# A field-pair product kernel: w loaded in 16 KB rows and turned on TensorE, columns split over both array halves, first three tiles interleaved, five stores a tile

One core of one Trainium2 chip. The metric is the device time of one execution in microseconds (us), the median of several; lower is better.

## The reference

```python
# inputs: (4096, 32, 64) float32, W: (496, 64, 64) float32
idx_i, idx_j = np.triu_indices(32, k=1)          # 496 pairs i < j
vi = inputs[:, idx_i, :]
vj = inputs[:, idx_j, :]
vidots = jnp.einsum('bpd,pde->bpe', vi, W)
return vidots * vj                               # (4096, 496, 64) float32
```

The output is 520 MB; the inputs x and w are 33.6 MB and 8.1 MB. The kernel is above all a stream of stores.

## The kernel before

The batch lies on the partitions, 128 samples a tile, 32 tiles. A field i has 31 - i pairs, so one i is a [64] x [64, (31 - i) * 64] product and a multiply with a contiguous slice of x. Fields 2k and 2k + 1 lie in the two halves of the contraction rows. w is loaded with d on the partitions, so that its contiguous pieces are rows of 64 floats (256 B).

```python
opool = ctx.enter_context(tc.tile_pool(name="opool", bufs=4))
psum = ctx.enter_context(tc.tile_pool(name="psum", bufs=4, space=bass.MemoryType.PSUM))
# ... w of field 2k in partitions 0-63 and of field 2k + 1 in 64-127
eng.dma_start(
    out=wt[s * D : (s + 1) * D, :n, :],
    in_=w[p0[i] : p0[i] + n].rearrange("p d e -> d p e"),
)
# ... for each tile t, group g of field couples, couple k
nc.tensor.matmul(
    ps[:, a : a + m, :],
    xT[t][s * D : (s + 1) * D, k, :],
    wts[k][s * D : (s + 1) * D, c0 + a : c0 + a + m, :],
    start=True, stop=True,
)
# ...
nc.vector.tensor_mul(
    ot[:, o : o + n, :], ps[:, :n, :], xs[t][:, j : j + n, :]
)
# ... once a group
nc.sync.dma_start(
    out=out[t * P : (t + 1) * P, base : base + total, :],
    in_=ot[:, :total, :],
)
```

Of the kernel before, what the change touches and what calls it, by code (L numbers as in the profile page):

```python
# [1 line left out]

# [5 lines left out]

F32 = mybir.dt.float32


@with_exitstack
def kernel(
    ctx: ExitStack,
    tc: tile.TileContext,
    x: bass.AP,
    w: bass.AP,
    out: bass.AP,
):
    """out[b, p, :] = (x[b, i, :] @ w[p]) * x[b, j, :], p running over the pairs i < j.  # L20

    The batch lies on the partitions. The pairs of one i are contiguous in w and
    out, and their j are contiguous in x, so one i is one [64] x [64, (31 - i) * 64]
    product and one elementwise multiply. Fields 2k and 2k + 1 sit in the lower and
    upper half of the contraction rows, whose matmuls run side by side.
    """
    nc = tc.nc

    B, F, D = x.shape
    P = 128  # L30
    assert 2 * D == P and F % 2 == 0 and B % P == 0
    NT = B // P
    NK = F // 2
    BANK = 512 // D  # pairs in one PSUM bank
    CH = 2 * BANK  # pairs in one PSUM tile
    p0 = [i * (F - 1) - i * (i - 1) // 2 for i in range(F)]  # first pair of field i

    # Runs of field couples that share a store.
    groups, run = [], []
    for k in range(NK):  # L40
        n = p0[2 * k + 1] - p0[2 * k] + (F - 2 - 2 * k)
        if run and sum(m for _, m in run) + n > 2 * F + 2:
            groups.append(run)
            run = []
        run.append((k, n))
    groups.append(run)
    cap = max(sum(m for _, m in g) for g in groups)

    const = ctx.enter_context(tc.tile_pool(name="const", bufs=1))
    xpool = ctx.enter_context(tc.tile_pool(name="xpool", bufs=3))  # L50
    xtpool = ctx.enter_context(tc.tile_pool(name="xtpool", bufs=2))
    opool = ctx.enter_context(tc.tile_pool(name="opool", bufs=4))
    psum = ctx.enter_context(tc.tile_pool(name="psum", bufs=4, space=bass.MemoryType.PSUM))

    ident = const.tile([P, P], F32, tag="ident", name="ident")
    make_identity(nc, ident)

    def load_x(t: int):
        xs = xpool.tile([P, F, D], F32, tag="xs", name=f"xs_{t}")
        nc.scalar.dma_start(out=xs, in_=x[t * P : (t + 1) * P])  # L60
        return xs

    def transpose_x(t: int, xs):
        xT = xtpool.tile([P, NK, P], F32, tag="xT", name=f"xT_{t}")
        for h in range(NK // 8):
            pt = psum.tile([P, 8, P], F32, tag="ps", name=f"pt_{t}_{h}")
            for c in range(8):
                k = 8 * h + c
                nc.tensor.transpose(pt[:, c, :], xs[:, 2 * k : 2 * k + 2, :], ident)  # L69
            nc.scalar.copy(xT[:, 8 * h : 8 * h + 8, :], pt)  # L70
        return xT

    xs = {0: load_x(0)}

    # w of field 2k in partitions 0-63 and of field 2k + 1 in 64-127.
    wts = []
    for k in range(NK):
        wt = const.tile([P, F - 1 - 2 * k, D], F32, tag=f"w{k}", name=f"w_{k}")
        for s in range(2):
            i = 2 * k + s  # L80
            n = F - 1 - i
            if n:
                eng = nc.sync if s == 0 else nc.scalar
                eng.dma_start(  # L84
                    out=wt[s * D : (s + 1) * D, :n, :],
                    in_=w[p0[i] : p0[i] + n].rearrange("p d e -> d p e"),
                )
        wts.append(wt)

    xs[1] = load_x(1)  # L90
    xT = {0: transpose_x(0, xs[0])}

    for t in range(NT):
        if t + 2 < NT:
            xs[t + 2] = load_x(t + 2)
        for g, grp in enumerate(groups):
            if g == len(groups) // 2 and t + 1 < NT:
                xT[t + 1] = transpose_x(t + 1, xs[t + 1])
            base = p0[2 * grp[0][0]]
            total = sum(m for _, m in grp)  # L100
            ot = opool.tile([P, cap, D], F32, tag="ot", name=f"ot_{t}_{g}")
            for k, _ in grp:
                for c0 in range(0, F - 1 - 2 * k, CH):
                    live = []
                    for s in range(2):
                        n = min(CH, F - 1 - 2 * k - s - c0)
                        if n > 0:
                            ps = psum.tile([P, CH, D], F32, tag="ps", name=f"ps_{t}_{k}_{c0}_{s}")
                            live.append((s, n, ps))
                    for a in range(0, CH, BANK):  # L110
                        for s, n, ps in live:
                            m = min(BANK, n - a)
                            if m > 0:
                                nc.tensor.matmul(  # L114
                                    ps[:, a : a + m, :],
                                    xT[t][s * D : (s + 1) * D, k, :],
                                    wts[k][s * D : (s + 1) * D, c0 + a : c0 + a + m, :],
                                    start=True,
                                    stop=True,
                                )  # L120
                    for s, n, ps in live:
                        i = 2 * k + s
                        o = p0[i] + c0 - base
                        j = i + 1 + c0
                        nc.vector.tensor_mul(  # L125
                            ot[:, o : o + n, :], ps[:, :n, :], xs[t][:, j : j + n, :]
                        )
            nc.sync.dma_start(
                out=out[t * P : (t + 1) * P, base : base + total, :],
                in_=ot[:, :total, :],  # L130
            )
        del xs[t], xT[t]


# [1 line left out]
_INS = ["r_inputs", "L0_rec_W"]  # L136
_OUTS = [((4096, 496, 64), "float32")]


# [20 lines left out]
```

## Time and profile before

The time before was 1375.78 us, median of three (1375.63 to 1375.88). Its profile:

| | before |
|---|---|
| span of the profiled run | 1374.4 us |
| TensorE busy | 1282.8 us (93%) |
| VectorE busy | 1170.1 us (85%) |
| ScalarE busy | 64.9 us |
| instructions; TensorE matmul records | 13,479; 5,376 |
| first store issued | 53.5 us |
| store, issue to landing (median, 300 to 1250 us) | 11.2 us |
| VectorE's last multiply ends | 1365.6 us |

TensorE has the highest share, and that misleads: a busy share is an average, and an engine that is always handed work in time can look busy without setting the end. The pair to read is the rate of the DMA engines over time and the tile time. A *tile time* in this text is the distance between the same instruction in two successive tiles; averages over tiles 8 to 28 are taken from VectorE's first multiplies. It was 41.28 us. The DMA share adds up the times of all packets, so it can be over 1: it was 1.35 between 10 and 40 us in this kernel, which means that packets of one engine overlap in time.

### The profile page before, as it was taken

Reading aid. Unit: us, or ns where it says so; the run is one execution under the profiler, and the core shown is the slowest. Engines: PE = TensorE matmul, PEld = TensorE weight load, DVE = VectorE, ACT = ScalarE, POOL = GpSimd, SP = SyncE. Lnnn points to the kernel's source line nnn. Section 1 sums busy time; section 2 is a strip of 40 time slices with the busy share of each in tenths; the row PEclk is TensorE's granted clock in tenths of the full one; section 3 lists DMA queues with packets and bytes.
Section 4 is the critical chain, followed back from the end, with each engine's and each line's share of the span. In section 5 each row is a group of like instructions: output and inputs, shape, how many; then the busy total and the mean of one; then the engine's idle time right before and its main releaser. Section 6 shows DMA issues by size and latency. Waiting matters only on the chain.

```text
span 1374.4 us, 13479 instructions
## 1 busy us (share of the span) xinstructions
PE 1282.8 (93%) x5376; PEld 646.9 (47%) x5376; DVE 1170.1 (85%) x1472; ACT 64.9 (5%) x65; POOL 0.7 (0%) x6
## 2 busy tenths in 40 slices
PE   1699999999999999999999999999999999999997
PEld 0344444544444545444545444544444544444543
DVE  0588888998898898898888888988888988888987
ACT  0100000000000000000000000000000000000000
POOL 0000000000000000000000000000000000000000
PEclk6799999999999999999999999999999999999999
DMA  9999999999999999999999999999999999999999
GB/s 213 295 392 419 432 419 420 421 419 418 429 421 420 420 421 416 431 416 418 420 417 398 431 419 420 422 420 418 430 416 420 419 418 418 430 415 420 404 393 386
DMA packets 82990, 562.65 MB, mean 409 GB/s; under 512 B 37872, under 2 KB 37872, under 8 KB 41968
## 3 DMA queue, kind: packets, MB, share of 16 engines
q1 hardware_dynamic: 62720, 524.31, 92.5%
q10 hardware_dynamic: 20208, 37.49, 7.7%
q8 instruction: 42, 0.69, 0.2%
q14 instruction: 20, 0.16, 0.0%
HBM read 41.68 MB, written 520.09 MB: 409 GB/s over the span
## 4 chain that ended last, share of the span: by engine, by line
PE 78%; DVE 12%; DMA 5%; ACTq 2%; issue 2%; ACT 0%; DVEq 0%
PE ps L114 74%; DVE ot L125 12%; PE pt L69 4%; DMA out_dram<-ot 4%; ACTq L84 2%; DMA w<-in_L_rec_W_dram 1%; ACT xT L70 0%; ACTq L60 0%; ACT L70 0%; DVEq L125 0%; DVEq L156 0%
## 5 line engine op out<-in xcount | busy, mean ns | idle before, releaser
L125 DVE TENSOR_TENSOR ot<-ps,xs 128x1024 f32<-128x1024 f32 (+15 forms) x1472 | 1170.1, 866 | 195.5 <-PE ps L114 192.4
L114 PE MATMUL ps<-w,xT 64*128 64x512 f32 (+6 forms) x4864 | 1217.4, 540 | 75.9 <-DVE ot L125 40.1
L114 PEld LDWEIGHTS ps<-w,xT 64*128 64x128 f32 x4864 | 590.5, 186 | 689.3 <-DVE ot L125 426.9
L70 ACT COPY xT<-pt 128x1024 f32<-128x1024 f32 x64 | 63.6, 1013 | 1199.8 <-PE pt L69 1160.2
L69 PE MATMUL pt<-ident,xs 128*128 128x128 f32 x512 | 69.6, 284 | 6.4 <-DMA xs<-in_r_inputs_dram 6.3
L69 PEld LDWEIGHTS pt<-ident,xs 128*128 128x128 f32 x512 | 56.4, 143 | 28.9 <-DVE ot L125 22.6
L70 ACT ACT_TABLE_LOAD x1 | 1.3, 1283 | 42.4 <-DMA w<-in_L_rec_W_dram 42.4
masks.py:199 POOL TENSOR_SCALAR_AFFINE_SELECT ident<-ident 128x128 f32<-128x128 f32 x1 | 0.3, 292 | 0.1
masks.py:197 POOL MEMSET ident<- 128x128 f32 x1 | 0.2, 204 | 0.3 <-POOLq L147 0.3
L147 POOL MEMSET const-bfloat16-1.0<- 128x1 bf16 x1 | 0.1, 101 | 0.0
L147 POOL MEMSET const-uint8-127<- 128x1 uint8 x1 | 0.1, 101 | 0.0
L147 POOL MEMSET const-float32-0.0<- 128x1 f32 x1 | 0.1, 98 | 0.2 <-issue 0.2
L147 POOL MEMSET const-float32-1.0<- 128x1 f32 x1 | 0.1, 98 | 0.0
## 6 DMA issues: line engine op xcount, KB each, us to landing
out_dram<-ot SPq DMA_DIRECT2D x32, 2016.0 KB, 10.8
out_dram<-ot SPq DMA_DIRECT2D x32, 1984.0 KB, 9.2
out_dram<-ot SPq DMA_DIRECT2D x32, 1952.0 KB, 10.5
out_dram<-ot SPq DMA_DIRECT2D x32, 1824.0 KB, 11.0
out_dram<-ot SPq DMA_DIRECT2D x32, 1696.0 KB, 11.4
out_dram<-ot SPq DMA_DIRECT2D x32, 1568.0 KB, 11.6
out_dram<-ot SPq DMA_DIRECT2D x32, 1440.0 KB, 11.8
out_dram<-ot SPq DMA_DIRECT2D x32, 1312.0 KB, 9.8
```

The lines of the kernel that those rows point to most:

```text
L69: nc.tensor.transpose(pt[:, c, :], xs[:, 2 * k : 2 * k + 2, :], ident)
L70: nc.scalar.copy(xT[:, 8 * h : 8 * h + 8, :], pt)
L84: eng.dma_start(out=wt[s * D : (s + 1) * D, :n, :], in_=w[p0[i] : p0[i] + n].rearrange("p d e -> d p e"),)
L114: nc.tensor.matmul(ps[:, a : a + m, :], xT[t][s * D : (s + 1) * D, k, :], wts[k][s * D : (s + 1) * D, c0 + a : c0 + a + m, :], start=True, ...
L125: nc.vector.tensor_mul(ot[:, o : o + n, :], ps[:, :n, :], xs[t][:, j : j + n, :])
L147: nc = _bacc.Bacc("TRN2", target_bir_lowering=False, num_devices=1)
```

## The change

The change has these parts:

- w comes with pairs on the partitions (16 KB rows, four chunks of up to 128 pairs) and TensorE turns it. VectorE, GpSimd and ScalarE first copy the columns apart with a stride (for the later chunks GpSimd alone).
- The even and odd halves of the array no longer hold two fields, but the two halves of the columns e of one field; so one multiply serves a whole field, and any run of fields can share a store.
- Five stores a tile, of 90 to 106 pairs each, replace the smaller groups; three output buffers instead of four, three PSUM buffers instead of four.
- The first three tiles are taken block by block in turn, so that w is needed more slowly while it arrives.
- x of tiles 1 and 2 is loaded on SyncE's queue, behind the first chunk of w; x of later tiles on ScalarE's, asked for at the end of the tile whose buffer it takes.

```diff
+    def load_w(c: int):
+        raw[c] = rpool.tile([P, D * D], F32, tag="raw", name=f"raw_{c}")   # one buffer
+        nc.sync.dma_start(out=raw[c][: b - a, :], in_=wflat[a:b])
+    def turn_w(c: int, k: int, copy):
+        src = raw[c][:r, :].rearrange("p (d h e) -> p e h d", h=2, d=D)
+        copy(rp[:r], src[:, k * EP : (k + 1) * EP])
+        if k == E2 // EP - 1 and c + 1 < len(wrows):
+            load_w(c + 1)
+        # ... 8 transposes by nc.tensor.transpose, 2 evictions by nc.scalar.copy
...
-    opool = ctx.enter_context(tc.tile_pool(name="opool", bufs=4))
+    opool = ctx.enter_context(tc.tile_pool(name="opool", bufs=3))
...
+    groups = [[(0, 3)], [(3, 5), (5, 7)], [(7, 9), (9, 11)], [(11, 14), (14, 17)],
+              [(17, 20), (20, 23), (23, 26), (26, 29), (29, 31)]]
+    blocks = [(t, g) for g in range(len(groups)) for t in range(NX)]      # NX = 3
+    blocks += [(t, g) for t in range(NX, NT) for g in range(len(groups))]
...
+                for k in range(E2 // EP):      # a later chunk c of w, four parts k
+                    due.setdefault(s - 18 + 4 * k, []).append(("w", c, k))
+    engines = [nc.vector.tensor_copy, nc.gpsimd.tensor_copy, nc.scalar.copy, nc.vector.tensor_copy]
...
+                for h in range(2):
+                    rows = slice(h * D, (h + 1) * D)
+                    nc.tensor.matmul(ps[:, h, lo - pa : hi - pa, :],
+                        xT[t, r][rows, i - r[0] + 1 - h, :],
+                        wT[c][rows, lo - a : hi - a, :], start=True, stop=True)
...
+            if g == len(groups) - 1 and t + NX < NT:
+                load_x(t + NX, nc.scalar)
```

More of the change, by code (lines that the diff above doesn't have):

```diff
@@ L30 @@
     P = 128
-    assert 2 * D == P and F % 2 == 0 and B % P == 0
+    assert 2 * D == P and B % P == 0
     NT = B // P
-    NK = F // 2
-    BANK = 512 // D
-    CH = 2 * BANK
+    NP = F * (F - 1) // 2
+    E2 = D // 2
+    BANK = 512
+    CH = BANK // E2
     p0 = [i * (F - 1) - i * (i - 1) // 2 for i in range(F)]
-    groups, run = [], []
-    for k in range(NK):
-        n = p0[2 * k + 1] - p0[2 * k] + (F - 2 - 2 * k)
-        if run and sum(m for _, m in run) + n > 2 * F + 2:
-            groups.append(run)
-            run = []
-        run.append((k, n))
@@ L46 @@
-    groups.append(run)
-    cap = max(sum(m for _, m in g) for g in groups)
-    const = ctx.enter_context(tc.tile_pool(name="const", bufs=1))
-    xpool = ctx.enter_context(tc.tile_pool(name="xpool", bufs=3))
-    xtpool = ctx.enter_context(tc.tile_pool(name="xtpool", bufs=2))
-    opool = ctx.enter_context(tc.tile_pool(name="opool", bufs=4))
-    psum = ctx.enter_context(tc.tile_pool(name="psum", bufs=4, space=bass.MemoryType.PSUM))
+    groups = [
+        [(0, 3)],
+        [(3, 5), (5, 7)],
+        [(7, 9), (9, 11)],
+        [(11, 14), (14, 17)],
+        [(17, 20), (20, 23), (23, 26), (26, 29), (29, 31)],
+    ]
@@ new lines @@
+    RUN = max(b - a for g in groups for a, b in g) + 1
+    cap = max(p0[g[-1][1]] - p0[g[0][0]] for g in groups)
+    cuts = [*range(0, NP, P), NP]
+    wrows = list(zip(cuts[:-1], cuts[1:]))
+    NX = 3
+    const = ctx.enter_context(tc.tile_pool(name="const", bufs=1))
+    rpool = ctx.enter_context(tc.tile_pool(name="rpool", bufs=1))
+    ppool = ctx.enter_context(tc.tile_pool(name="ppool", bufs=2))
+    xpool = ctx.enter_context(tc.tile_pool(name="xpool", bufs=NX))
+    xtpool = ctx.enter_context(tc.tile_pool(name="xtpool", bufs=6))
@@ L55 @@
+    opool = ctx.enter_context(tc.tile_pool(name="opool", bufs=3))
+    psum = ctx.enter_context(tc.tile_pool(name="psum", bufs=3, space=bass.MemoryType.PSUM))
+    tpsum = ctx.enter_context(tc.tile_pool(name="tpsum", bufs=2, space=bass.MemoryType.PSUM))
     ident = const.tile([P, P], F32, tag="ident", name="ident")
     make_identity(nc, ident)
-    def load_x(t: int):
-        xs = xpool.tile([P, F, D], F32, tag="xs", name=f"xs_{t}")
-        nc.scalar.dma_start(out=xs, in_=x[t * P : (t + 1) * P])
-        return xs
@@ L63, in transpose_x @@
-    def transpose_x(t: int, xs):
-        xT = xtpool.tile([P, NK, P], F32, tag="xT", name=f"xT_{t}")
-        for h in range(NK // 8):
-            pt = psum.tile([P, 8, P], F32, tag="ps", name=f"pt_{t}_{h}")
-            for c in range(8):
-                k = 8 * h + c
-                nc.tensor.transpose(pt[:, c, :], xs[:, 2 * k : 2 * k + 2, :], ident)
-            nc.scalar.copy(xT[:, 8 * h : 8 * h + 8, :], pt)
-        return xT
-    xs = {0: load_x(0)}
-    wts = []
-    for k in range(NK):
-        wt = const.tile([P, F - 1 - 2 * k, D], F32, tag=f"w{k}", name=f"w_{k}")
-        for s in range(2):
-            i = 2 * k + s
-            n = F - 1 - i
-            if n:
-                eng = nc.sync if s == 0 else nc.scalar
-                eng.dma_start(
-                    out=wt[s * D : (s + 1) * D, :n, :],
-                    in_=w[p0[i] : p0[i] + n].rearrange("p d e -> d p e"),
-                )
-        wts.append(wt)
@@ L90 @@
-    xs[1] = load_x(1)
-    xT = {0: transpose_x(0, xs[0])}
-    for t in range(NT):
-        if t + 2 < NT:
-            xs[t + 2] = load_x(t + 2)
-        for g, grp in enumerate(groups):
-            if g == len(groups) // 2 and t + 1 < NT:
-                xT[t + 1] = transpose_x(t + 1, xs[t + 1])
-            base = p0[2 * grp[0][0]]
-            total = sum(m for _, m in grp)
-            ot = opool.tile([P, cap, D], F32, tag="ot", name=f"ot_{t}_{g}")
-            for k, _ in grp:
-                for c0 in range(0, F - 1 - 2 * k, CH):
-                    live = []
-                    for s in range(2):
-                        n = min(CH, F - 1 - 2 * k - s - c0)
-                        if n > 0:
-                            ps = psum.tile([P, CH, D], F32, tag="ps", name=f"ps_{t}_{k}_{c0}_{s}")
-                            live.append((s, n, ps))
-                    for a in range(0, CH, BANK):
-                        for s, n, ps in live:
-                            m = min(BANK, n - a)
-                            if m > 0:
-                                nc.tensor.matmul(
-                                    ps[:, a : a + m, :],
-                                    xT[t][s * D : (s + 1) * D, k, :],
-                                    wts[k][s * D : (s + 1) * D, c0 + a : c0 + a + m, :],
-                                    start=True,
-                                    stop=True,
-                                )
-                    for s, n, ps in live:
-                        i = 2 * k + s
-                        o = p0[i] + c0 - base
-                        j = i + 1 + c0
-                        nc.vector.tensor_mul(
-                            ot[:, o : o + n, :], ps[:, :n, :], xs[t][:, j : j + n, :]
-                        )
@@ new lines, with load_x @@
+    xs = {}
+    def load_x(t: int, eng):
+        xs[t] = xpool.tile([P, F + 1, D], F32, tag="xs", name=f"xs_{t}")
+        nc.gpsimd.memset(xs[t][:, 0, :], 0.0)
+        eng.dma_start(out=xs[t][:, 1:, :], in_=x[t * P : (t + 1) * P])
+    wflat = w.rearrange("p d e -> p (d e)")
+    raw = {}
+    wT = [
+        const.tile([P, b - a, E2], F32, tag=f"w{c}", name=f"wT_{c}")
+        for c, (a, b) in enumerate(wrows)
+    ]
+    EP = 8
+    EU = BANK // P
+    def load_w(c: int):
+        a, b = wrows[c]
+        raw[c] = rpool.tile([P, D * D], F32, tag="raw", name=f"raw_{c}")
+        nc.sync.dma_start(out=raw[c][: b - a, :], in_=wflat[a:b])
@@ new lines, in turn_w @@
+    def turn_w(c: int, k: int, copy):
+        r = wrows[c][1] - wrows[c][0]
+        rp = ppool.tile([P, EP, 2, D], F32, tag="rp", name=f"rp_{c}_{k}")
+        src = raw[c][:r, :].rearrange("p (d h e) -> p e h d", h=2, d=D)
+        copy(rp[:r], src[:, k * EP : (k + 1) * EP])
+        if k == E2 // EP - 1 and c + 1 < len(wrows):
+            load_w(c + 1)
+        for u in range(0, EP, EU):
+            e0 = k * EP + u
+            pt = tpsum.tile([P, EU, P], F32, tag="pt", name=f"ptw_{c}_{e0}")
+            for n in range(EU):
+                nc.tensor.transpose(
+                    pt[:, n, :r],
+                    rp[:r, u + n].rearrange("p h d -> p (h d)"),
+                    ident[:r, :r],
+                )
+            nc.scalar.copy(
+                wT[c][:, :, e0 : e0 + EU], pt[:, :, :r].rearrange("p e r -> p r e")
+            )
@@ new lines, in turn_x @@
+    def turn_x(t: int, a: int, b: int):
+        pt = tpsum.tile([P, RUN, P], F32, tag="pt", name=f"ptx_{t}_{a}")
+        for n in range(b - a + 1):
+            nc.tensor.transpose(
+                pt[:, n, :],
+                xs[t][:, a + n : a + n + 2, :].rearrange("p f d -> p (f d)"),
+                ident,
+            )
+        xT = xtpool.tile([P, RUN, P], F32, tag="xT", name=f"xT_{t}_{a}")
+        nc.scalar.copy(xT[:, : b - a + 1, :], pt[:, : b - a + 1, :])
+        return xT
+    load_x(0, nc.scalar)
@@ new lines @@
+    load_w(0)
+    for t in range(1, NX):
+        load_x(t, nc.sync)
+    blocks = [(t, g) for g in range(len(groups)) for t in range(NX)]
+    blocks += [(t, g) for t in range(NX, NT) for g in range(len(groups))]
+    steps = [
+        (t, g, r, i, c0, min(CH, F - 1 - i - c0))
+        for t, g in blocks
+        for r in groups[g]
+        for i in range(*r)
+        for c0 in range(0, F - 1 - i, CH)
+    ]
+    AHEAD = 6
+    due: dict = {}
+    seen = set()
+    for s, (t, g, r, i, c0, m) in enumerate(steps):
+        if (t, r) not in seen:
+            seen.add((t, r))
+            due.setdefault(max(0, s - AHEAD), []).append(("x", t, r))
+        for c, (a, b) in enumerate(wrows):
+            if c and a < p0[i] + c0 + m and c not in seen:
+                seen.add(c)
+                for k in range(E2 // EP):
+                    due.setdefault(s - 18 + 4 * k, []).append(("w", c, k))
@@ new lines @@
+    engines = [nc.vector.tensor_copy, nc.gpsimd.tensor_copy, nc.scalar.copy, nc.vector.tensor_copy]
+    for k in range(E2 // EP):
+        turn_w(0, k, engines[k])
+    xT = {}
+    ot = None
+    for s, (t, g, r, i, c0, m) in enumerate(steps):
+        for what, *args in due.get(s, ()):
+            if what == "x":
+                tt, rr = args
+                xT[tt, rr] = turn_x(tt, *rr)
+            else:
+                turn_w(*args, nc.gpsimd.tensor_copy)
+        base, end = p0[groups[g][0][0]], p0[groups[g][-1][1]]
+        pa = p0[i] + c0
+        if pa == base:
+            ot = opool.tile([P, cap, D], F32, tag="ot", name=f"ot_{t}_{g}")
+        ps = psum.tile([P, 2, CH, E2], F32, tag="ps", name=f"ps_{s}")
+        for c, (a, b) in enumerate(wrows):
+            lo, hi = max(pa, a), min(pa + m, b)
+            if lo < hi:
+                for h in range(2):
+                    rows = slice(h * D, (h + 1) * D)
+                    nc.tensor.matmul(
+                        ps[:, h, lo - pa : hi - pa, :],
+                        xT[t, r][rows, i - r[0] + 1 - h, :],
+                        wT[c][rows, lo - a : hi - a, :],
+                        start=True,
+                        stop=True,
+                    )
+        o = pa - base
+        j = i + 1 + c0
+        nc.vector.tensor_mul(
+            ot[:, o : o + m, :].rearrange("p m (h e) -> p m h e", h=2),
+            ps[:, :, :m, :].rearrange("p h m e -> p m h e"),
+            xs[t][:, j + 1 : j + 1 + m, :].rearrange("p m (h e) -> p m h e", h=2),
+        )
+        if pa + m == end:
@@ L128 @@
             nc.sync.dma_start(
-                out=out[t * P : (t + 1) * P, base : base + total, :],
-                in_=ot[:, :total, :],
-            )
-        del xs[t], xT[t]
+                out=out[t * P : (t + 1) * P, base:end, :],
+                in_=ot[:, : end - base, :],
+            )
+            if g == len(groups) - 1 and t + NX < NT:
+                load_x(t + NX, nc.scalar)
 _INS = ["r_inputs", "L0_rec_W"]
```

## The prediction

(Cut from the text were terms of its sums: what stands beside the 7.5 us of the first loads to make 9.6 us; a time for GpSimd's strided copy, inside the "about 10 us" and between the second chunk's landing at 22 to 23 us and steps 2 to 5 at 26; and a least time for TensorE's small steps, inside the 28.4 us. With them the first store came to 30 us, and the total to 30 + 1322 + 4 - 1 = 1355 us.)

> **What bounds the kernel now.** I read the page first, then the stretches, the waits and the chain of waits. From the page, DMA share and rate in 40 slices of 34.4 us, and the DMA queues:
>
> ```profile
> DMA  9999999999999999999999999999999999999999
> GB/s 213 295 392 419 432 419 420 421 419 418 429 421 420 420 421 416 431 416 418 420 417 398 431 419 420 422 420 418 430 416 420 419 418 418 430 415 420 404 393 386
> ...
> q8 instruction: 42, 0.69, 0.2%
> ...
> HBM read 41.68 MB, written 520.09 MB: 409 GB/s over the span
> ```
>
> The DMA engines are busy everywhere, but at half rate for the first 40 us. Stretches of the span (busy us of PE, weight loads, VectorE, ScalarE, GpSimd, then granted clock, DMA share, GB/s):
>
> ```profile
> 10.00:40.00 30.00, 0.00 (x0) 0.00 (x0) 0.00 (x0) 0.00 (x0) 0.00 (x0) 0.55 1.35 213
> 40.00:54.00 14.00, 9.28 (x29) 4.33 (x30) 5.03 (x5) 3.21 (x3) 0.00 (x0) 0.62 0.71 196
> 200.00:400.00 200.00, 194.26 (x825) 98.16 (x821) 177.74 (x223) 9.88 (x10) 0.00 (x0) 1.00 1.01 422
> 800.00:1200.00 400.00, 387.39 (x1634) 194.68 (x1632) 355.23 (x447) 19.92 (x20) 0.00 (x0) 1.00 1.01 421
> ```
>
> Two regimes: until about 54 us w comes in and nothing computes; afterwards the 16 engines are full at 421 GB/s. The first store is issued at 53.5 us in the timeline.
>
> The waits (us in total, times, longest):
>
> ```profile
> DVE ot L125 <- PE ps L114: 192.4, 130, 48.5
> ...
> DVE ot L125 <- DMA out_dram<-ot: 2.0, 2, 1.1
> ```
>
> VectorE's timeline of one tile (start, us, what, idle time before it and what ended it):
>
> ```profile
> 213.41 19.11 DVE L125 TENSOR_TENSOR ot<-ps,xs 128x1024 f32<-128x1024 f32 x20 [1.48 <-PE ps L114]
> 234.62 3.08 DVE L125 TENSOR_TENSOR ot<-ps,xs 128x1024 f32<-128x1024 f32 x4 [2.10 <-PE ps L114]
> 238.20 2.36 DVE L125 TENSOR_TENSOR ot<-ps,xs 128x1024 f32<-128x1024 f32 x2 [0.50 <-PE ps L114]
> ```
>
> VectorE is busy 1170.1 / 32 = 36.6 us a tile and waits about 4.5 us for TensorE, so compute alone has a tile time of about 41.1 us. It hardly ever waits for a store, although the DMA engines are full. From the chain of waits, the same place in successive tiles:
>
> ```profile
> 207.41 12.02 PE ps L114 x46
> 248.49 12.03 PE ps L114 x46
> ...
> 1114.78 12.03 PE ps L114 x46
> 1156.04 12.03 PE ps L114 x46
> ```
>
> Tiles first follow each other at 41.08 us, later at 41.26. In between, the time from issue to landing of a store creeps from 9 to 12.4 us and stays there (the fourth buffer is then the limit). So compute wants 41.08 and DMA allows about 41.25: the two are balanced, and **a faster compute gains nothing; only bytes per us, or DMA time not used, can be won.**
>
> [...]
> 1. [...]w in 256 B pieces ran at 213 GB/s; a 16,128 B row takes 601 ns and a 7,168 B row 272 ns (medians of the packets), that is 36.7 ns per KB (435.7 GB/s over 16 engines) plus 8.8 ns a row.
> 2. [...]TensorE's 2 x 5376 instructions are 42 blocks, queue q8 has 42 packets. They took about 0.93 us each beside stores.
> 3. [...]around the 16 transposes there are 0.17 us before the second starts and 0.20 us before the next matmul, against 0.109 us between transposes.
> 4. [...]No strided GpSimd copy is in this trace.
>
> **The change, part by part.**
>
> *Start, removed.* w as 256 B pieces: 8.13 MB at 213 GB/s, about 40 us; and 53.5 us to the first store.
>
> *Start, added.* Now x0 (1.05 MB) and the first 128 rows of w (2.1 MB) come at full rate: 3.15 MB / 0.42 = 7.5 us[...] so about 9.6 us. Then this chunk is turned in four parts: a strided copy (VectorE, GpSimd, ScalarE, VectorE), 8 transposes, two ScalarE evictions of 512 (about 0.6 us each, from 1.013 us for 1024). ScalarE's eight evictions and its copy are 6 us, [...]and only two staging buffers exist, so parts wait for each other: about 10 us, so the first product near 20 us. The second chunk of w has a single raw buffer and is asked for only when the last copy has read the first (about 16 us); it lands at 22 to 23 us,[...] and TensorE, in order, is due to transpose it before step 2. So steps 2 to 5 run from about 26 and **the first store leaves at about 30 us, against 53.5.** Here 23 us are won. But by then 7.3 MB have been moved instead of 11.3 MB: w chunks 3 and 4 (4 MB, 9.5 us of DMA time) now travel among stores.
>
> *First three tiles.* TensorE there has 46 steps a tile. A full step (4 records) is 0.854 us,[...] which sums to 28.4 us plus 1 us for the steps cut at w's chunks. Twelve turns of x are about 0.7 us each (4 x 0.109 plus the two gaps above), 8.4 us. So 38 us a tile, and 3 x 4.8 us more for w. Against it the DMA needs about 126 us from 30 us on: TensorE is slightly behind. I put 4 us of idle DMA time to it.
>
> *Steady state.* VectorE: still 46 multiplies of 31,744 elements, 36.6 us[...]. TensorE 38 us with only three PSUM buffers; gaps where a turn of x meets small steps (the tile start worst, about 1.7 us) sum to 3.7 us. Compute: 36.6 + 3.7 = 40.3 us, slightly better than 41.08. DMA: 5 rows instead of 10 per partition and tile save 5 x 8 x 8.8 ns = 0.35 us if a row of 23 to 27 KB stays one packet. TensorE's stream grows: 98 matmuls in two records and 43 transposes are 239 a tile against 168, so about 61 blocks instead of 42. Each block is 0.61 us of one DMA engine by the fit above; in the landing marks of a store late in the run one engine is 1 to 2 us behind the other fifteen, as if one engine carried these blocks. Then it loses (61 - 42) x 0.61 / 32 = 0.36 us more a tile. The two cancel: **about 41.2 us a tile, as before.** The multiplies, the halves and the store count gain nothing on the path.
>
> *Sum.* Before, from the first store to the end: 1374.4 - 53.5 = 1320.9 us for 561.77 - 11.3 = 550.5 MB, 416.8 GB/s all in. After, 554.4 MB remain at 30 us. At 416.8 that is 1330 us; at 420 (without the before kernel's uneven first tiles and thin tail, which a queue full to the end avoids) 1320. I take 1322, and 4 us of idle: 30 + 1322 + 4 = 1356. Subtracting 1 us for the chance of a cheaper row: **1355 us, 1.5% less.**
>
> **Rivals.**
> - *Rows pay off, fetches don't hurt.* If long rows stay whole and the instruction blocks are spread over engines, the tile falls to about 40.8 us, 11 us less: 1343. For: the 8.8 ns a row is clean in the packets. Against: stores land when their slowest engine does, and one lags already.
> - *Compute becomes the bound.* [...]40.3 becomes over 41.5: at 42 us, 29 tiles give some 20 us back: about 1375. For: [...]three buffers instead of four. Against: turns are issued six steps early, and DVE has 4.5 us of slack to lose first.
> - *The start is better tuned than I think.* If the second chunk arrives before TensorE asks, the first store leaves at 25 us: 1350.
> - *The start is worse.* If GpSimd's strided copies take 5 us, TensorE stalls on each part of chunk 2 and the first stores leave 10 us later: 1365.
>
> **Range and chances.** The sum says 1355; the 2% line is at 1348.3. Row saving or a quick start alone nearly reach it, both would pass it; compute as bound would take it all back, hardly more. Range 1341 to 1372. Faster by over 2%: 0.28; within: 0.67; slower: 0.05.
>
> **What would show it.** GB/s in the first slice: near 300, no 213 plateau. First store at 28 to 32 us, TensorE waiting for the GpSimd copy of chunk 2 just before. In the middle: DMA full at 419 to 422 GB/s, tile time 41.0 to 41.4, and VectorE now really waiting for stores. Queue q8: about 61 packets. VectorE's multiplies: 36.6 us a tile. I am wrong if the rate in the middle exceeds 425 GB/s (rows), if DMA shows gaps there while VectorE waits for TensorE (compute), or if the first store is outside 25 to 35 us.

## The result, and the profile after

The changed kernel took **1370.58 us**, median of four (1370.23 to 1372.98); the kernel before beside it took 1375.70 us (1374.94 to 1375.88). The ratio is 0.9967, with a 95% interval of 0.9953 to 0.9981: by the 2% line the same, and really, if barely, faster. (All ratios here are the mean time of one kernel's fast runs over that of the other's of the same rounds, so not quite the ratio of the medians quoted. Runs of different sets are compared by their ratios.) The forecast was 1355 us: the class and the range held it, but of a forecast gain of 21 us only 5 came.

| | before | after |
|---|---|---|
| first store issued | 53.5 us | 35.5 us |
| tile time, tiles 8 to 28 | 41.28 us | 41.39 us |
| VectorE's last multiply ends | 1365.6 us | 1356.5 us |
| span | 1374.4 us | 1370.6 us |
| store, issue to landing (median) | 11.2 us | 16.1 us |
| TensorE busy; its matmul records | 1282.8 us; 5,376 | 1292.4 us; 7,776 |
| VectorE busy | 1170.1 us | 1183.4 us |

From the page of the changed kernel, DMA share and rate in 40 slices of 34.3 us, and the DMA queues:

```profile
DMA  5999999999999999999999999999999999999998
GB/s 214 382 406 405 410 430 432 431 424 419 410 422 428 414 416 421 414 425 419 415 421 414 419 425 423 416 397 426 424 423 418 410 416 418 422 427 417 421 404 354
...
q8 instruction: 61, 1.00, 0.3%
...
HBM read 41.68 MB, written 520.09 MB: 410 GB/s over the span
```

The bytes and, within 1 GB/s, the mean rate are as before. The first slice moves about as much as before (214 against 213 GB/s), but for another reason: before, the engines were busy at half rate; now they run at full rate and stand idle for nearly half of the slice. (The prediction looked for near 300 GB/s here; that missed.) The stretches of the changed kernel show that (busy us of PE, weight loads, VectorE, ScalarE, GpSimd; granted clock, DMA share, GB/s):

```profile
0.00:20.00 20.00, 6.08 (x32) 4.74 (x32) 2.05 (x2) 6.83 (x9) 3.76 (x10) 1.00 0.74 279
20.00:40.00 20.00, 16.89 (x68) 9.08 (x68) 8.75 (x8) 4.49 (x9) 7.64 (x4) 0.83 0.42 181
40.00:80.00 40.00, 40.00 (x213) 21.27 (x213) 32.39 (x33) 10.27 (x20) 7.79 (x4) 1.00 1.00 383
...
200.00:1300.00 1100.00, 1055.80 (x6339) 544.17 (x6341) 980.03 (x1220) 171.78 (x318) 3.93 (x26) 1.00 0.99 420
1340.00:1372.00 32.00, 15.84 (x111) 8.97 (x107) 15.63 (x24) 2.82 (x5) 0.00 (x0) 0.78 0.77 328
```

Read them in three parts. At the start, the DMA share of 0.42 between 20 and 40 us is the hole in front of the first store; then, from 40 to 80 us, TensorE is busy for 40.00 of 40.00 us. The DMA share is 1.00 there too, but VectorE waits 5.7 us for TensorE and never for a store, so TensorE is the limit. In the middle the DMA engines are full, and the rate is 420 GB/s. At the end the rate falls to 328. The same stretch before, to its own end, did better:

```profile
1340.00:1375.00 35.00, 24.64 (x98) 11.28 (x94) 24.36 (x35) 0.00 (x0) 0.00 (x0) 0.90 0.91 381
```

Both stretches reach a little past the end of their span. Over exactly the last 32 us of each span the shares are 0.81 after and 0.91 before, which is 6.1 us of idle DMA time at the end against 2.9 us.

VectorE's waits after (us in total, times, longest):

```profile
DVE ot L186 <- PE ps L177: 99.8, 150, 5.5
DVE ot L186 <- DMA out_dram<-ot: 50.1, 48, 2.3
```

Before it waited 2.0 us for stores in all. Now it waits 50.1 us, some 1.6 us a tile: the DMA engines set the pace openly, and compute has slack. In the chain of waits the stores lie where only TensorE lay before (start, length, what):

```profile
456.53 16.09 DMA out_dram<-ot
...
497.95 16.07 DMA out_dram<-ot
...
539.36 16.09 DMA out_dram<-ot
```

The distances are 41.42 and 41.41 us. The start in the timeline (start, us, what, idle time before it and what ended it):

```profile
17.55 0.33 SPq L88 DMA_DIRECT2D raw<-in_L_rec_W_dram  x1
...
22.66 3.42 DVE L186 TENSOR_TENSOR ot<-ps,xs 128x1024 f32<-128x1024 f32 x3 [5.19 <-PE ps L177]
...
25.85 3.77 POOL L94 COPY rp<-raw 128x1024 f32<-128x1024 f32 x2 [11.67 <-DMA raw<-in_L_rec_W_dram]
...
27.79 1.97 PE L101 MATMUL ptw<-ident,rp 128*128 128x128 f32 x8 [2.77 <-POOL rp L94]
...
31.59 1.09 DVE L186 TENSOR_TENSOR ot<-ps,xs 128x896 f32<-128x896 f32 x1 [5.50 <-PE ps L177]
...
35.48 0.35 SPq L192 DMA_DIRECT2D out_dram<-ot  x1
```

Read it from the bottom. VectorE's gap of 5.50 us before its fourth multiply is TensorE standing for 2.77 us and then turning w; TensorE stood for GpSimd's copy of the second chunk; GpSimd stood 11.67 us for that chunk, which was asked for at 17.55 us and was there at 25.85.

### The profile page after: what moved, and what is told of

It is laid out like the page before. It is cut to its first block, busy times and chain, and to the rows that moved or that the text cites. A ratio compares the mean times of both kernels' runs of the same rounds, so it can differ in the third digit from the quotient of the medians.

```text
span 1370.6 us, 18821 instructions
## 1 busy us (share of the span) xinstructions
PE 1292.4 (94%) x7776; PEld 675.2 (49%) x7776; DVE 1183.4 (86%) x1474; ACT 227.5 (17%) x418; POOL 31.4 (2%) x51
## 2 busy tenths in 40 slices
DMA packets 28292, 562.97 MB, mean 411 GB/s; under 512 B 3136, under 2 KB 3136, under 8 KB 3136
## 4 chain that ended last, share of the span: by engine, by line
PE 50%; DMA 32%; DVE 16%; issue 1%; POOL 0%; DVEq 0%; POOLq 0%; SPq 0%
PE ps L177 38%; DMA out_dram<-ot 31%; DVE ot L186 16%; PE ptx L114 10%; DMA raw<-in_L_rec_W_dram 1%; PE ptw L101 1%; DVE rp L94 0%; POOL rp L94 0%; DVEq L186 0%; POOLq L94 0%; SPq L88 0%; DVEq L94 0%
## 5 line engine op out<-in xcount | busy, mean ns | idle before, releaser
L186 DVE TENSOR_TENSOR ot<-ps,xs 128x1024 f32<-128x1024 f32 (+7 forms) x1472 | 1181.3, 868 | 157.7 <-PE ps L177 99.8
L177 PE MATMUL ps<-wT,xT 64*128 64x512 f32 (+13 forms) x6272 | 1090.8, 467 | 46.9 <-DVE ot L186 44.5
L177 PEld LDWEIGHTS ps<-wT,xT 64*128 64x128 f32 x6272 | 515.4, 186 | 509.3 <-DVE ot L186 302.0
L120 ACT COPY xT<-ptx 128x512 f32<-128x512 f32 (+1 forms) x384 | 207.5, 541 | 1088.7 <-PE ptx L114 1086.3
L114 PE MATMUL ptx<-ident,xs 128*128 128x128 f32 x1376 | 240.9, 290 | 0.2 <-ACT wT L106 0.2
L114 PEld LDWEIGHTS ptx<-ident,xs 128*128 128x128 f32 x1376 | 144.5, 141 | 145.6 <-issue 138.5
L101 PE MATMUL ptw<-ident,rp 128*128 128x128 f32 (+1 forms) x128 | 20.5, 304 | 16.6 <-DVE rp L94 12.5
L101 PEld LDWEIGHTS ptw<-ident,rp 128*128 128x128 f32 (+1 forms) x128 | 15.6, 156 | 26.0 <-issue 16.1
L94 POOL COPY rp<-raw 128x1024 f32<-128x1024 f32 (+1 forms) x13 | 26.0, 2018 | 74.0 <-DMA raw<-in_L_rec_W_dram 32.1
L106 ACT COPY wT<-ptw 128x512 f32<-128x512 f32 (+1 forms) x32 | 17.4, 574 | 35.7 <-PE ptw L101 35.7
```

What stands on the lines that cost most here:

```text
L94: copy(rp[:r], src[:, k * EP : (k + 1) * EP])
L101: nc.tensor.transpose(pt[:, n, :r], rp[:r, u + n].rearrange("p h d -> p (h d)"), ident[:r, :r],)
L106: nc.scalar.copy(wT[c][:, :, e0 : e0 + EU], pt[:, :, :r].rearrange("p e r -> p r e"))
L114: nc.tensor.transpose(pt[:, n, :], xs[t][:, a + n : a + n + 2, :].rearrange("p f d -> p (f d)"), ident,)
L120: nc.scalar.copy(xT[:, : b - a + 1, :], pt[:, : b - a + 1, :])
L177: nc.tensor.matmul(ps[:, h, lo - pa : hi - pa, :], xT[t, r][rows, i - r[0] + 1 - h, :], wT[c][rows, lo - a : hi - a, :], start=True, stop= ...
```

## The experiments

Twelve kernels ran, in three sets, each set on one chip beside the kernel before. Unless said otherwise, each is an edit of the changed kernel.

**Do instruction blocks cost DMA time?** The theory: every block of instructions that TensorE fetches (a packet of 16,384 B on queue q8: 61 of them for 2 x 7,776 records of TensorE, matmuls and weight loads, after, 42 for 2 x 5,376 before, so about 256 records each) is carried by a DMA engine that the stores wait for, so the longer program pays back what the fewer rows save. The rivals: compute sets the tile time, or one DMA engine is slow whatever it carries. e1 shortens TensorE's stream with bfloat16 operands (3,442 matmul records between 200 and 1200 us instead of 5,763; the products have one record instead of two). e2 and e3 put it back with small dummy matmuls that the real one then overwrites.

```diff
# e1_bf16
-        const.tile([P, b - a, E2], F32, tag=f"w{c}", name=f"wT_{c}")
+        const.tile([P, b - a, E2], BF16, tag=f"w{c}", name=f"wT_{c}")
-        xT = xtpool.tile([P, RUN, P], F32, tag="xT", name=f"xT_{t}_{a}")
+        xT = xtpool.tile([P, RUN, P], BF16, tag="xT", name=f"xT_{t}_{a}")
# e2_bf16_fill1 and e3_bf16_fill3, besides: range(1) in e2, range(3) in e3
+                    for _ in range(1):
+                        nc.tensor.matmul(ps[:, h, lo - pa : lo - pa + 1, :],
+                            xT[t, r][rows, i - r[0] + 1 - h, :],
+                            wT[c][rows, lo - a : lo - a + 1, :], start=True, stop=True)
```

> Wrong result on purpose (w and x are rounded to bf16 when they are evicted): each matmul is one record and one weight load instead of two and two, so TensorE has 282 instructions a tile instead of 478, 36 fetch blocks instead of 61, and is far from being a bound. Theory (one DMA engine also carries TensorE's instruction blocks, 0.62 us each, and stores land when that engine is done): tile time in the middle 40.23 + 36 x 0.617 / 32 = 40.9 us instead of 41.4, total about 1355. Rival A (one DMA engine is slow by itself, whatever the instructions): tile time stays 41.4, total about 1367 (only the start gains). Rival B (TensorE or VectorE sets the tile time): it falls to about 37 to 38 us wherever the DMA lets it.

> As e1, plus one matmul of 32 columns ahead of each real one, into the place that the real one overwrites: 478 instructions a tile and 61 blocks again, with TensorE still far from a bound. Theory: tile time back at 41.4 us, total about 1368. Rival A: 41.4 in e1 and here alike, no difference between e1 and e2. Rival B: no difference to e1.

> As e2 with three small matmuls ahead of each: 870 instructions a tile, about 110 blocks. Theory: tile time 40.23 + 110 x 0.617 / 32 = 42.35 us, total about 1397, the lag of the last DMA engine larger still. Rivals A and B: as e2 (B: unless TensorE gets close to 40 us of work a tile, which would show as VectorE waiting for it).

Measured: e1 1359.76 us, 0.9879 (0.9865 to 0.9894); e2 1374.52 us, 0.9986 (0.9971 to 1.0001); e3 1399.39 us, 1.0170 (1.0154 to 1.0185). I had expected e1 to fail the comparison with the reference; with rounded operands it passed all the same. Successive stores in the chain of waits, first e1:

```profile
543.46 16.19 DMA out_dram<-ot
584.44 16.17 DMA out_dram<-ot
```

then e2:

```profile
590.79 17.03 DMA out_dram<-ot
...
632.17 17.02 DMA out_dram<-ot
```

and e3:

```profile
557.27 17.38 DMA out_dram<-ot
...
599.51 17.36 DMA out_dram<-ot
```

The distances are 40.98, 41.38 and 42.24 us, with a store as the link each time. With the blocks of the instruction queue (q8):

| | blocks | tile time, tiles 8 to 28 |
|---|---|---|
| e1 | 36 | 40.99 us |
| e2 | 61 | 41.41 us |
| the changed kernel, float32 | 61 | 41.39 us |
| e3 | 110 | 42.28 us |

e3 against e1 is 1.29 us a tile for (110 - 36) / 32 = 2.31 blocks a tile: **0.56 us a block**, near the 0.61 that the prediction had from the packets. And e2, with one record a product and dummies, is where the float32 kernel is with the same number of blocks. TensorE's work differs between the two, and the number of blocks doesn't. That rules out compute as what sets the tile time, and a DMA engine that is slow by the same amount whatever the instructions.

The totals of e1 and e2 came 5 and 6 us above the expected 1355 and 1368 us. Their first three tiles were done at 162.8 and 164.8 us, later than the changed kernel's 160.5, although TensorE has less to do there.

Two things keep the theory from being shown. The dummies add instructions and blocks together, so the cost may belong to either. And the packets of the traces speak against the path that the theory gave. A packet's record doesn't say which engine carried it, but in a busy stretch nearly every packet starts 3 or 4 ns before another one ends, so the packets of one engine can be strung together from their times (no view of the profile shows this). Between 300 and 1250 us the changed kernel has 43 block packets. Most were found on the engines whose landing mark comes second to fourth from last, and none on the engine that lands last. That last engine is slow in its own rows instead (median times of a row of 27,136 B):

| | blocks | on the engine that lands last | on an engine in the middle |
|---|---|---|---|
| e1 | 36 | 1028 ns | 1006 ns |
| the changed kernel | 61 | 1047 ns | 1006 ns |
| e2 | 61 | 1048 ns | 1006 ns |
| e3 | 110 | 1076 ns | 1006 ns |

Over the 40 rows that an engine has in a tile, all sizes together, the excess is 0.86, 1.33 and 2.08 us in e1, e2 and e3. Its steps, 0.47 and 0.75 us, are near those of the tile time, 0.42 and 0.87. So a longer instruction stream of TensorE goes with slower rows on one engine, and that engine carries next to none of the blocks. How the one causes the other is open.

**Is one engine the bottleneck, and which?** A store of rows 0 to 119 was meant to leave one of 16 engines out, and one of rows 0 to 7 to load only some of them. No run here shows which engine takes which rows; the totals that stand in each are its outcomes by which engine lags.

```diff
# e4_split15: five of the 160 stores
+            halves = [(0, 120), (120, P)] if g == 1 and t % 6 == 0 and t else [(0, P)]
+            for q0, q1 in halves:
+                nc.sync.dma_start(out=out[t * P + q0 : t * P + q1, base:end, :],
+                    in_=ot[q0:q1, : end - base, :])
# e10_extra8: from tile 3 one extra store of rows 0 to 7 a tile
+            for q in (P, 8) if g == 1 and t >= NX else (P,):
+              nc.sync.dma_start(out=out[t * P : t * P + q, base:end, :],
+                  in_=ot[:q, : end - base, :])
```

> The changed kernel with one store in every 30 (five in all) cut into rows 0 to 119 and 120 to 127 of the tile. [...]tile time about 40.4 us, total about 1345. [...]5 us slower than the changed kernel. If another: the same, 1371.

> The changed kernel, from tile 3 on with one more store a tile: rows 0 to 7 of its second store again, same bytes to the same place, 8 rows of 27 KB[...]. [...]1.0 us more a tile, tile time 42.4, total about 1400. [...]no change, 1371[...].

Measured: e4 1437.65 us, 1.0452 (1.0434 to 1.0469); e10 1497.65 us, 1.0879 (1.0862 to 1.0895). From the issues of e4 (count, KB each, us from issue to landing):

```profile
out_dram<-ot SPq DMA_DIRECT2D x27, 3392.0 KB, 16.9
...
out_dram<-ot SPq DMA_DIRECT2D x5, 3180.0 KB, 30.1
```

The store with 8 rows fewer takes 30.1 us to land, not 16.9. Its rows of 27,136 B took up to 2.08 and 2.35 us each (95th and 99th percentile of these packets), against a median of 1.006 us. In e10 the rows of that size took up to 2.99 and 3.66 us, and each extra store of eight rows cost about 127 / 29 = 4.4 us. Why these rows take so long is not shown. Both runs failed in their purpose: the disturbance is larger than the effect, and **which engine lags stays open**.

**Do the fewer rows pay?** e5 issues each store as two halves of the columns; e8 gives the kernel before five stores a tile.

```diff
# e5_stores10
+            mid = (base + end) // 2
+            for q0, q1 in [(base, mid), (mid, end)]:
+                nc.sync.dma_start(out=out[t * P : (t + 1) * P, q0:q1, :],
+                    in_=ot[:, q0 - base : q1 - base, :])
# e8_before_5stores: an edit of the kernel before
-        if run and sum(m for _, m in run) + n > 2 * F + 2:
+        if run and sum(m for _, m in run) + n > 118:
-    opool = ctx.enter_context(tc.tile_pool(name="opool", bufs=4))
+    opool = ctx.enter_context(tc.tile_pool(name="opool", bufs=3))
```

> The changed kernel with each of its stores issued as two of half the columns at the same moment: 10 rows instead of 5 per partition and tile, all else as it is. Theory (every DMA engine pays 8.8 ns a row and the lagging one decides): 5 x 8 x 8.8 ns = 0.35 us more a tile, tile time 41.75, total about 1381 against 1370.6. Rival (the row cost falls on engines that wait anyway, or is hidden): 1371.

> The kernel before with 5 stores a tile (up to 118 pairs) from 3 buffers, and nothing else of the change. Theory: its DMA tile time falls from 41.25 to about 40.9 us, under the 41.08 us that its compute takes, so compute sets it: tile time 41.08, and the first store is larger and leaves 4 us later: total 1371 to 1375, VectorE never waiting for a store. Rival (only DMA time counts): 41.25 - 0.35 = 40.9, total about 1365.

Measured: e5 1376.18 us, 0.9999 (0.9984 to 1.0014). Its tile time is 41.77 us, 0.38 over the changed kernel's 41.39; five rows more for each of eight partitions of an engine, at 8.8 ns, are 0.35. So the row saving is real. The total rose by less than I expected (0.9999 against 0.9967, some 4 us instead of 10), because a half may go as soon as its own columns are done: the first store left at 26.8 us instead of 35.5. That was an accident of the experiment that gave an idea for later.

e8 took 1375.50 us, 0.9992 (0.9975 to 1.0009). Its chain of waits, the same place in successive tiles:

```profile
125.42 12.03 PE ps L114 x46
...
166.51 12.03 PE ps L114 x46
...
207.61 12.03 PE ps L114 x46
```

Tiles follow each other at 41.09 and 41.10 us, and at 41.10 on average over tiles 8 to 28, with TensorE as the link and no wait of VectorE for a store. So the first reading in the prediction was right: compute of the kernel before wants 41.1 us and stores of ten rows allow 41.25 to 41.3. Fewer rows alone gain only what lies between, and here the larger first store, out at 57.7 us instead of 53.5, gives it back.

**What is the start worth?** Two kernels move the second chunk of w, and one takes the interleaving away.

```diff
# e6_late_w1: the four parts of a later chunk are turned 4, 3, 2 and 1 steps later
-                    due.setdefault(s - 18 + 4 * k, []).append(("w", c, k))
+                    due.setdefault(s - 14 + 3 * k, []).append(("w", c, k))
# e7_early_w1: the second chunk is loaded at once, into a free output buffer
+        if c == 1:
+            raw[c] = opool.tile([P, cap * D], F32, tag="ot", name=f"raw_{c}")[:, : D * D]
+    load_w(1)
+                    due.setdefault(s - 20 + 3 * k if c == 1 else s - 18 + 4 * k, []).append(("w", c, k))
# e9_no_interleave
-    blocks = [(t, g) for g in range(len(groups)) for t in range(NX)]
-    blocks += [(t, g) for t in range(NX, NT) for g in range(len(groups))]
+    blocks = [(t, g) for t in range(NT) for g in range(len(groups))]
-                    due.setdefault(s - 18 + 4 * k, []).append(("w", c, k))
+                    due.setdefault(s - 4 + k, []).append(("w", c, k))
```

> The changed kernel with the four parts of w's second chunk turned ahead of steps 6, 9, 12, 15 instead of 2, 6, 10, 14 (and the later chunks likewise 14, 11, 8, 5 steps ahead of use). Theory (TensorE, in order, stands before step 2 until that chunk has come and GpSimd has copied it): steps 2 to 5 run at once, first store at about 29 us instead of 35.5, total 4 to 6 us less, about 1365. Rival (the first store is late for the engines' own work, or what is won is lost again before the DMA queue is full): within 2 us of the changed kernel.

> The changed kernel with w's second chunk loaded at once into a store buffer that is idle then, and turned ahead of steps 0, 3, 6, 9; the third chunk is then asked for at about 17 us. Theory: no stall before step 2, first store at about 30 us, and 2.1 MB more moved before it (5 us): total about 1360. Rival: as in e6, no more than 2 us gained.

> The changed kernel without the interleaving of the first three tiles: tile by tile, each chunk of w turned in the four steps before its use. Theory (the interleaving buys time to bring and turn w while stores run): the first tile waits for chunks 2, 3, 4 one after the other, about 16 us each (8 us load, 4 GpSimd copies of 2 us), so it takes about 75 us instead of 40, the DMA engines idle for some 20 us more, total about 1388. Rival (the start hardly matters, since everything after it is bound by the DMA engines and buffers catch up): 1371.

Measured: e6 1368.59 us, 0.9941 (0.9926 to 0.9955), and e7 1368.65 us, 0.9941 (0.9926 to 0.9956): each about 0.26% or 3.6 us better than the changed kernel's 0.9967, with intervals that just touch its own. For e6 that is a little under the 4 to 6 us of the theory and over the 2 us of the rival. Its first store left at 30.6 us. Its timeline:

```profile
24.09 6.48 DVE L186 TENSOR_TENSOR ot<-ps,xs 128x1024 f32<-128x1024 f32 x6 [6.48 <-PE ps L177]
...
32.28 3.42 DVE L186 TENSOR_TENSOR ot<-ps,xs 128x1024 f32<-128x1024 f32 x3 [1.72 <-PE ps L177]
```

VectorE now has six multiplies in a row where it had three and a gap of 5.50 us: the gap was indeed TensorE's, turning w in its fixed order before it was needed. e7 had its first store at 32.2 us and a DMA share of 0.93 instead of 0.74 in the first 20 us, but 0.90 between 40 and 80 us, where the changed kernel had 1.00. I had expected 1360 us, and that missed: bytes moved earlier do not help where TensorE makes the output. In these three kernels TensorE is full from about 40 us on (over 19 us busy in nearly every 20, up to 160 us), and the phase of the first three tiles ended at 160.5 us in the changed kernel, 157.0 in e6 and 156.1 in e7.

e9 took 1381.78 us, 1.0035 (1.0020 to 1.0050). Its stretch from 60 to 80 us, columns as above:

```profile
60.00:80.00 20.00, 15.70 (x78) 9.52 (x80) 6.53 (x9) 5.34 (x10) 7.64 (x4) 0.74 0.47 183
```

A single tile needs all of w at once and waits for it: half of the DMA time of this stretch is idle. The interleaving is worth 1.0035 - 0.9967 = 0.68%, about 9 us; I had expected 17.

**Can it be made faster?** e11 puts the ideas together: later turning of w, all four first copies on VectorE (see below why), its evictions shared by VectorE and ScalarE, and the first stores of the three first tiles in halves. e12 adds float32r operands, which like bfloat16 gave the products one record instead of two (3,136 on its page against 6,272 of the changed kernel).

```diff
# e11_best
+            evict = nc.vector.tensor_copy if c == 0 and e0 // EU % 2 else nc.scalar.copy
+                    due.setdefault(s - 14 + 3 * k, []).append(("w", c, k))
+    engines = [nc.vector.tensor_copy] * 4
+            parts = [(base, mid), (mid, end)] if t < NX and g == 0 else [(base, end)]
# e12_best_fp32r, besides
-        const.tile([P, b - a, E2], F32, tag=f"w{c}", name=f"wT_{c}")
+        const.tile([P, b - a, E2], F32R, tag=f"w{c}", name=f"wT_{c}")
-        xT = xtpool.tile([P, RUN, P], F32, tag="xT", name=f"xT_{t}_{a}")
+        xT = xtpool.tile([P, RUN, P], F32R, tag="xT", name=f"xT_{t}_{a}")
```

> The changed kernel with a quicker start: all four copies of the first chunk on VectorE, its evictions alternating between VectorE and ScalarE, the later chunks turned 14, 11, 8, 5 steps ahead (as e6), and the first stores of the three interleaved tiles issued in halves. Theory: first store at about 23 us instead of 35.5, first three tiles TensorE-bound and done about 10 us earlier, tile time unchanged at 41.4: total about 1361. Rival (what is won at the start is lost before 160 us): no better than e6, 1368.

> As e11, with the products in the float32r type[...], which should need one record and one weight load a matmul as bf16 did: 36 fetch blocks, TensorE no bound at the start either. Theory: tile time 40.9, first three tiles bound by VectorE and the DMA: total about 1345, over 2% under the kernel before. Correctness is open; if it needs two records like float32, it is as e11.

The reason for VectorE is in the page of the changed kernel, the strided copies of w (count, busy us, mean ns):

```profile
L94 POOL COPY rp<-raw 128x1024 f32<-128x1024 f32 (+1 forms) x13 | 26.0, 2018 | 74.0 <-DMA raw<-in_L_rec_W_dram 32.1
...
L94 DVE COPY rp<-raw 128x1024 f32<-128x1024 f32 x2 | 2.1, 1026 | 15.4 <-DMA raw<-in_L_rec_W_dram 11.4
L94 ACT COPY rp<-raw 128x1024 f32<-128x1024 f32 x1 | 1.9, 1945 | 0.0
```

VectorE takes half as long as the other two. Yet e11 took 1368.85 us, 0.9940 (0.9926 to 0.9955), no better than e6: its first store (a half) left at 26.6 us, but VectorE's first multiply began at 23.13 us, no earlier than 22.66, and the three-tile phase ended at 156.4 us, as in e6 and e7. There TensorE is the limit again. The expected 1361 us missed. e12 took **1358.36 us, 0.9863 (0.9847 to 0.9880)**, with 36 blocks and 41.00 us a tile, and passed the comparison. Its tile time was as expected, its total not: 1345 us had been the forecast. Its stretches, columns as above:

```profile
120.00:160.00 40.00, 31.35 (x141) 19.62 (x139) 27.97 (x44) 8.14 (x15) 0.30 (x2) 0.54 0.84 342
...
200.00:1300.00 1100.00, 964.09 (x3789) 533.13 (x3788) 993.34 (x1235) 174.41 (x322) 3.93 (x26) 0.54 1.00 423
```

In the middle it moves 423 GB/s against 420. What still is lost: 16% of the DMA time between 120 and 160 us, where all three x buffers come free together and the next x has to be waited for (4.9 us on TensorE). With its TensorE no longer full, the phase of the first three tiles still ended at 161.0 us, later than e11's 156.4: VectorE now waited 3.6 us for a store and 4.6 us for turns of w, besides that x. So behind TensorE other limits stand close by at the start; they have not been taken apart. It is the best kernel measured, at the price of operands cast to float32r; in full float32, e6, e7 and e11 are equally good at 0.994.

## Why the prediction was right or wrong

*What bounds the kernel* was right. e8, in which compute sets 41.10 us a tile, and the waits for stores after the change both show that the two limits lay within 0.2 us of each other. One reading was loose: "until about 54 us w comes in and nothing computes" has TensorE busy for 9.28 us from 40 us on in its own line.

*Start, added* was mis-sized, by 5.5 us. The prediction had the first store at 30 us and named the second chunk of w as the reason; it left at 35.5, just outside the stated 25 to 35, for that reason. The chunk was asked for at 17.55 us (I had said 16) and was there 8.3 us later, not 6 to 7; then its copy, its turns and VectorE's second gap came one after another. e6 took 4.9 of the 5.5 us away by letting TensorE multiply first. GpSimd's copy took 2.0 us, less than the 3 to 4 us that the forecast left between the chunk's landing and steps 2 to 5, so the copy was not to blame.

*First three tiles*: TensorE as the limit there was right, and more so than thought. Its work was summed to 3 x 38 + 3 x 4.8 = 128 us, and it was busy for 135.6 us between 20 and 160 us. (The 0.7 us for a turn of x is too small by its own terms: 4 x 0.109 and the two gaps make 0.81.) The prediction charged 4 us of idle time to it, but drew no conclusion on what an earlier first store would be worth: e6, e7 and e11 brought it out 3 to 9 us earlier and all ended this phase only 3.5 to 4.4 us earlier.

*Steady state* was right in its sizes, but not in its path. Long rows stay whole (a row of 27,136 B is one packet of 1.006 us, 27.136 x 36.7 + 8.8 = 1.005); the row saving is 0.38 us by e5 (0.35 predicted); there are 61 blocks; a block costs 0.56 us by e1 to e3 (0.61). But the reason given, one engine that carries the blocks and lands last, is not what the packets show (above: the last engine carried none of those found and was slow in its rows), so that the size came out right was in part luck. The sum of 41.2 us was 0.2 too low, and the cancelling isn't quite even: 41.28 went to 41.39. VectorE's multiplies are 1181.3 / 32 = 36.9 us a tile (36.6 predicted), and compute takes about 41.4 - 1.6 = 39.8 us (40.3).

*The sum* is where the prediction failed. The miss is 15.6 us: 5.5 before the first store, as said, and 10.1 after it, from this step: "at 420 (without the before kernel's uneven first tiles and thin tail, which a queue full to the end avoids) 1320. I take 1322". With the 4 us of idle and less 1 us for cheaper rows, that gave 1325 us from the first store on. It took 1370.6 - 35.5 = 1335.1 us; 554.4 MB in that time are 415.3 GB/s, less than the 416.8 of before. Of these 10 us, about 5.5 are the tile time, (41.39 - 41.2) x 29 tiles. The rest is mainly the tail, which the prediction took for gone: the DMA engines stood idle for 6.1 of the last 32 us, where before it was 2.9. The larger part of this is one engine: the last store's mark from it came at 1369.5 us, 3.7 us after the middle one's (1.7 us before). The time from VectorE's end to the span's end misleads here. It went from 8.8 to 14.1 us, but in e8, with larger stores and no other change but a buffer, it is 12.6 us with no more idle DMA time than before (0.91 over its last 32 us): a larger last store simply takes longer. In the landing marks of a store (one for each of 16 engines, 300 to 1250 us) the last engine comes 4.87 us after the middle one, against 3.20 before, and the second-last 1.40 against 1.31. One engine alone is late by that much, so at the end the others have nothing left to do. Fewer blocks shorten the lag only a little (4.24 us at 36 blocks in e1); in e8, where compute is the limit, it is 1.63 us. What makes that engine slow is open.

*Where the 23 us of the start went*, measured: the first store gained 18.0 us, and the time after it rose by 1335.1 - 1320.9 = 14.2 us. In this are 9.5 us for the two chunks of w that now travel among stores, as predicted (an estimate, 4 MB at 0.42 MB/us), about 3 us for the tile time (0.11 x 29) and about 3 for the idle time in the tail. These make 1 to 2 us more than the 14.2 measured; what the changed kernel did better elsewhere has not been separated.

Of the rivals, "rows pay off, fetches don't hurt" falls by e1 to e3, "compute becomes the bound" by VectorE's waits and e2. "The start is worse" is what happened, in half the size and for TensorE's order rather than slow copies; "better tuned" did not happen.

## What to carry to other kernels

When stores and compute are balanced, an earlier first store is worth only what the next limit lets through: here 18 us at the start became 5 at the end (9.5 of them went to bytes that only travel later), and 3 to 9 further us became 4. In a kernel bound by DMA, count the instructions too: here each block, about 256 more of TensorE's records, cost the stores 0.56 us (e1 to e3), by a path that is still open, and one record a product instead of two was worth more than the whole change (e1 0.9879 against 0.9967). Look at the tail by itself, at the DMA time that stands idle in it (6.1 of 32 us here), before you assume that a full queue makes it disappear.
